# An RWKV block on one core: three products of k and v move from GpSimd to VectorE, and the written order changes

## The chip, the core and the metric

The kernel runs on one core of one Trainium2 chip. A core has five engines that run side by side, each with a queue of its own that it works off in order: TensorE (PE in the profile; its weight loads are PEld), VectorE (DVE), ScalarE (ACT), GpSimd (POOL) and SyncE (SP), which here only issues DMA transfers. They wait for one another by semaphores. SBUF holds the tiles, PSUM what TensorE writes. The metric is the device time of one execution in microseconds (us); the median of the runs counts.

## The reference

One layer of an RWKV block over 8 batches of 256 tokens and 512 channels (32 heads of 16), in float32. Cut to what matters:

```python
xn = _ln(x, ln1_w, ln1_b)
sx = _token_shift(xn, state[:, i1])
...
x5 = xn[:, :, None] + sx[:, :, None] * (maa_stack + xxx)
w = exp(-exp(time_decay + tanh(x5[:, :, 1] @ decay_w1) @ decay_w2))
r, k, v = x5[:, :, 3] @ Wr.T, x5[:, :, 0] @ Wk.T, x5[:, :, 2] @ Wv.T
g = silu(x5[:, :, 4] @ Wg.T)

def step(s, rkvw):
    r_t, k_t, v_t, w_t = rkvw
    a = k_t[:, :, :, None] * v_t[:, :, None, :]
    out = einsum('bhk,bhkd->bhd', r_t, u * a + s)
    return (a + w_t[:, :, :, None] * s, out)

_, outs = scan(step, s0, (r, k, v, w))
att = group_norm(outs) * gn_w + gn_b
x = x + att * g @ Wo.T
...
x = x + sigmoid(xr @ ffn_Wr.T) * (square(relu(xk @ ffn_Wk.T)) @ ffn_Wv.T)
```

Each head carries a state of 16 x 16 values through the 256 tokens. The outer product `a` of k and v is what the change is about.

## The kernel before, in words

The work of a batch is cut into three stages. `inputs_of_scan` loads and normalizes x, mixes it with its shifted copy into the five inputs `x5` (tiles `mix`), and projects them to r, k, v, g and the decay w. `scan` runs the recurrence. `rest` normalizes the result, projects it with Wo and runs the second half of the layer. The last part of `rest` of one batch, the scans of the next and the projections of the one after that overlap in time.

`scan` works in 4 blocks of 128 channels, and each block in 4 steps, so 16 scans a batch and 128 in all. For each step a tile `vs` of 128 x 1024 is made: SyncE loads the v of a quarter of the block, spread over the partitions, from a copy `vo` of v in DRAM (L426); ScalarE puts the starting state into its first column (L964); VectorE multiplies it by k (L971). k is read from PSUM, where ScalarE has copied it (`kp`, L952). Then VectorE runs the recurrence over the 1024 columns in one scan instruction (L973), which reads the decay `wrep` that ScalarE has spread into PSUM (L954; there is one such buffer) and writes `st`. GpSimd multiplies `st` by r (L976), and when all four steps of a block are done, TensorE sums them over the channels in 16 small matmuls (L984, the gather of the block; its output is `pat`), and VectorE adds that to `att` (L990).

In batch 0 one product by k of each block but the first, that of the fourth step, is made by GpSimd instead (L968), which reads k from SBUF. These are the three of the title.

The order of the work is written out by hand. Each operation of each stage has a number, its place in one order over all engines, in the table `TURNS` of the class `Plan`: one row for the constants, 8 rows for the stage `inputs_of_scan`, 8 for `scan`, 8 for `rest`. `sequence` gives the numbers to the operations in the order in which the stage adds them, and `order` issues them by number, takes free buffers from the pools, and sorts by the start that it works out. For one engine the order of issue is so the order of the numbers.

`tiles` chooses how matmuls whose mode is `any` are cut: in four strips of 32 columns next to operations that need such strips (mode `columns`), otherwise whole. Other operations need tiles of 32 or 64 rows, or whole ones (`turn`). A change of the mode costs TensorE something, and so does a change between the activation tables of ScalarE (`exp` and `tanh`), for which the kernel issues a load (L1131).

Names in the text: `psd0` is the output of the projection to decay and gate inputs of batch 0, `psv0_0` that of the first half of v of batch 0, `xh` a normalized x before it is turned (L616), `xin` the input of the first mixing projection (L674 its half on ScalarE), `sx` the difference of x and its shifted copy, `cm` the mean of the state.

```python
for op in self.ops:
    for b in op.bufs:
...
while queue:
    op = self.ops[heapq.heappop(queue)[1]]
    at = max([free[op.engine], op.ready] + [b.since for b in op.bufs])
...
done.sort(key=lambda op: op.start)
```

Of the kernel before, what the change touches and what calls it, by code (L numbers as in the profile page):

```python
# [71 lines left out]
class Plan:  # L72
# [61 lines left out]
    def stage(self):  # L134
# [6 lines left out]
        17 61 12 44 62 72 60 96 59 114 112 113 228 73 13 16 22 25 109 131 132 149 21 18 38 41 42 46 40 45 70 39 43 47 69  # L141
        71 74,
        0 2 1 4 3 5 6 7 8 9 26 27 34 37 52 54 31 32 36 49 28 29 33 35 50 51 30 55 56 65 53 67 68 79 103 105 125 107 108
        136 80 82 85 106 134 139 75 76 78 87 84 86 120 77 81 83 133 135 140 130 100 126 137 138 127 129 157 160 161 187
        190 141 150 158 221 224 225 147 148 153 156 151 152 201 102 104 117 119 116 123 124 128 175 197 199 163 165 176
        236 237 240 269 299 335 256 257 275,
        10 11 15 14 19 23 20 24 48 89 88 90 92 93 94 142 91 95 97 110 155 144 146 164 174 177 183 191 194 238 245 263
        265 282 246 259 261 283 243 260 266 329 244 248 258 330 202 223 226 232 252 205 206 209 254 203 219 220 281 204
        207 208 345 300 306 331 328 336 397 399 403 413 414 301 302 339 309 312 332 340 343 344 351 355 380 349 352 348
        363 387 334 341 360 415 419 444 388 389 398 358 369 372 478 480 483 404 405 416,  # L150
        66 99 101 111 121 122 143 145 154 162 159 166 181 182 186 210 167 180 188 189 200 214 227 249 218 231 251 268
        284 406 429 431 436 449 420 421 434 459 450 451 462 487 428 433 441 460 373 374 383 386 443 378 381 392 458 375
        382 385 457 376 377 384 442 481 482 486 492 494 642 650 652 654 656 580 587 602 484 500 519 532 536 539 561 590
        594 535 537 540 556 557 498 511 526 639 641 657 499 523 527 589 640 669 648 649 755 683 695 746,
        603 618 631 632 633 634 635 637 645 646 647 658 684 686 694 696 655 675 679 680 685 705 711 718 692 717 725 736
        756 759 773 775 795 807 766 772 778 782 765 776 780 781 767 770 771 845 803 809 810 828 871 805 823 827 903 804
        808 817 821 818 819 820 822 898 907 908 910 911 1013 1021 1025 1053 1062 961 1003 1005 921 922 941 943 970 971
        957 999 1055 949 952 956 958 960 843 844 869 930 946 967 962 987 1018 855 878 879 1097 1103 1118 1058 1063 1099,
        672 697 693 701 706 708 721 722 739 814 863 865 870 895 923 815 937 963 1019 1020 1023 1059 745 935 959 1006
        1009 1054 1064 1060 1078 1079 1065 1077 1080 1119 1120 1149 1173 1174 1185 1221 1172 1183 1191 1210 1162 1167  # L160
        1168 1193 1170 1188 1190 1216 1127 1130 1139 1142 1233 1134 1136 1137 1220 1128 1132 1135 1152 1129 1131 1133
        1153 1282 1299 1301 1284 1294 1326 1333 1369 1357 1372 1283 1287 1302 1303 1304 1307 1305 1313 1319 1315 1320
        1327 1306 1317 1308 1318 1328 1202 1215 1244 1247 1253 1260 1340 1346 1354 1322 1341 1347 1390 1397 1428 1349
        1350 1424,
        1029 1138 1171 1187 1207 1217 1218 1229 1241 1243 1254 1263 1264 1281 1325 790 1331 1335 1348 1374 1378 1391
        1178 1330 1334 1370 1380 1387 1405 1410 1415 1435 1407 1408 1429 1438 1444 1500 1501 1505 1511 1566 1521 1523
        1527 1587 1515 1518 1535 1551 1517 1519 1528 1550 1455 1461 1464 1479 1565 1456 1457 1469 1475 1458 1463 1470
        1473 1460 1465 1480 1549 1599 1613 1615 1604 1612 1639 1642 1643 1644 1652 1626 1641 1649 1650 1672 1698 1667
        1668 1728 1743 1745 1796 1669 1671 1675 1677 1811 1561 1562 1600 1583 1625 1635 1670 1715 1716 1619 1624 1636
        2044 2046 2047 2036 2038 2087,  # L170
        1337 1336 1338 1339 1342 1520 1524 1525 1530 1552 1553 1554 1588 1590 1614 1559 1620 1648 1651 1689 1694 1699
        1433 1621 1640 1661 1662 1688 1702 1706 1707 1720 1714 1719 1722 1738 1741 1781 1793 1823 1843 1859 1794 1800
        1806 1821 1790 1795 1797 1820 1799 1804 1819 1861 1753 1767 1771 1779 1801 1772 1773 1780 1802 1754 1758 1759
        1832 1757 1761 1762 1860 1916 1919 1920 1933 1934 2013 2014 2015 2016 2043 1883 1884 1886 1839 1848 1851 1964
        1966 1972 1971 1975 2124 1965 1973 1995 2012 2078 1857 1867 1876 1954 1963 1981 1911 1915 1922 1987 2010 2042
        2190 2191 2205 2364 2374 2398,
        1679 1629 1695 1709 1710 1712 1717 1792 1831 1835 1856 1872 1874 1918 1921 1765 1930 1936 1937 1939 1949 1978
        1784 1924 1979 2003 2037 2040 2056 1982 2033 2045 2060 2061 2077 2080 2083 2092 2094 2101 2112 2131 2097 2100
        2110 2153 2096 2109 2119 2132 2095 2111 2127 2213 2134 2143 2155 2174 2231 2136 2140 2142 2186 2135 2137 2138
        2152 2139 2168 2177 2215 2247 2248 2250 2249 2252 2281 2293 2307 2291 2292 2253 2280 2282 2314 2339 2410 2479  # L180
        2482 2484 2487 2492 2503 2483 2485 2490 2494 2515 2171 2172 2192 2318 2321 2325 2254 2258 2276 2337 2368 2381
        2525 2530 2567 2519 2520 2540,
        58 63 98 185 253 267 276 277 286 287 293 294 307 308 278 279 285 288 295 296 297 298 313 168 172 169 170 171 173
        211 192 195 196 198 280 178 179 184 193 216 213 215 217 234 255 289 320 270 229 230 233 273 290 239 262 264 315
        322 235 242 250 310 311 212 222 247 274 291 325 326 346 241 305 321 292 316 318 327 356 271 303 317 324 354 272
        304 319 323 357 314 333 347 362 367 390 391 366 353 365 368 393 412 337 342 370 394 423 338 350 364 371 395 359
        379 396 411 424 438 447,
        57 64 118 427 425 439 544 545 553 562 564 568 570 574 546 547 554 555 558 565 566 573 591 361 418 432 400 426
        440 455 497 402 430 485 495 510 401 417 435 456 509 409 461 488 496 513 531 596 514 422 504 507 515 551 464 493
        506 517 548 463 505 508 549 550 410 452 479 563 572 588 620 599 445 559 567 530 560 576 595 612 604 606 608 621  # L190
        665 524 552 571 592 629 569 593 597 611 664 666 690 644 627 663 667 691 700 609 636 643 660 676 605 607 661 671
        689 529 638 659 677 699 730 731,
        408 437 453 764 747 824 866 867 880 883 884 888 893 917 885 886 887 904 905 914 915 916 919 534 682 710 703 714
        749 753 760 623 681 698 723 748 715 716 729 750 751 724 738 752 754 763 842 936 789 651 707 709 847 873 787 791
        801 846 872 768 774 796 800 813 737 757 779 825 874 920 940 944 662 864 881 851 868 875 901 912 848 849 876 894
        896 853 882 891 933 934 786 909 928 945 953 997 998 964 929 931 955 965 966 889 926 975 1011 1034 890 1001 1012
        1017 1044 950 974 976 977 1015 1045 1046,
        850 892 980 1022 948 1024 1036 1037 1042 1047 1048 1049 1051 1071 1206 1234 1235 1236 1237 1238 1239 1249 1072
        906 1008 1032 972 984 1031 1086 1094 1028 1033 1038 1085 1125 942 1026 1030 1039 1095 994 1004 1087 1088 1144
        1146 1147 1092 1052 1084 1096 1100 1111 1073 1102 1107 1154 1211 1091 1098 1106 1176 1212 1090 1101 1105 1110  # L200
        1186 1225 1268 1256 973 1198 1199 1184 1200 1205 1209 1258 1108 1208 1227 1231 1259 1195 1222 1228 1271 1274
        1181 1182 1204 1226 1285 1321 1329 1272 1232 1273 1278 1293 1323 1214 1240 1277 1355 1360 1158 1223 1275 1290
        1316 1230 1261 1276 1361 1362 1363 1379,
        1201 1279 1314 1384 1381 1385 1388 1389 1392 1393 1400 1401 1406 1420 1522 1539 1546 1555 1556 1557 1563 1598
        1452 1248 1356 1373 1265 1386 1412 1413 1449 1280 1351 1365 1411 1447 1345 1359 1367 1382 1448 1344 1352 1366
        1375 1431 1476 1478 1445 1376 1394 1414 1477 1548 1377 1436 1439 1450 1474 1395 1441 1442 1516 1558 1396 1440
# [1001 lines left out]
```

## Time and profile before

| | before |
|---|---|
| median of 3 runs | 605.23 us (605.15 to 607.45) |
| the profiled execution | 606.28 us |
| its span from the first to the last instruction | 604.5 us |
| TensorE busy | 594.1 us (98%) |
| VectorE busy | 537.9 us (89%) |
| ScalarE busy | 517.4 us (86%) |
| GpSimd busy | 508.5 us (84%) |
| transfers | 128.07 MB, mean 212 GB/s |
| table loads of ScalarE, line 1131 | 43 |

A row of the profile gives a line of the kernel (L973 is line 973), an engine, an operation, the tiles that it writes and reads, and times. In a timeline the first number is the start and the second the time up to the end of the last of the instructions that are merged in the row; the bracket is the idle time of the engine ahead of it and what ended it. Instructions on one engine overlap a little: the next starts before the one ahead has written its last columns. The granted clock of TensorE was 1.00 in all of the span, the higher of its two levels, 2.4 GHz.

### The profile page before, as it was taken

Reading aid. Unit: us, or ns where it says so; the run is one execution under the profiler, and the core shown is the slowest. Engines: PE = TensorE matmul, PEld = TensorE weight load, DVE = VectorE, ACT = ScalarE, POOL = GpSimd, SP = SyncE. Lnnn points to the kernel's source line nnn. Section 1 sums busy time; section 2 is a strip of 40 time slices with the busy share of each in tenths; the row PEclk is TensorE's granted clock in tenths of the full one; section 3 lists DMA queues with packets and bytes.
Section 4 is the critical chain, followed back from the end, with each engine's and each line's share of the span. In section 5 each row is a group of like instructions: output and inputs, shape, how many; then the busy total and the mean of one; then the engine's idle time right before and its main releaser. Section 6 shows DMA issues by size and latency. Waiting matters only on the chain.

```text
span 604.5 us, 19879 instructions
## 1 busy us (share of the span) xinstructions
PE 594.1 (98%) x8356; PEld 344.1 (57%) x8356; DVE 537.9 (89%) x500; ACT 517.4 (86%) x1207; POOL 508.5 (84%) x390
## 2 busy tenths in 40 slices
PE   8999999999999999999999999999999999999997
PEld 7576755466446754366653755465554464455464
DVE  5789999999999999998978999999999999995342
ACT  5898879999999899999999996999999989965440
POOL 1589999989999988999979997999999989897030
PEclk9999999999999999999999999999999999999999
DMA  9895677888999679959787897785999896945352
GB/s 301 280 249 137 170 184 198 238 209 219 233 267 264 190 220 226 241 133 265 193 243 206 255 280 204 186 213 127 281 230 206 233 255 188 275 152 174 93 187 71
DMA packets 55497, 128.07 MB, mean 212 GB/s; under 512 B 6112, under 2 KB 13680, under 8 KB 55408
## 3 DMA queue, kind: packets, MB, share of 16 engines
q1 hardware_dynamic: 51040, 122.61, 74.8%
q10 hardware_dynamic: 4368, 4.20, 2.1%
q8 instruction: 65, 1.06, 0.8%
q14 instruction: 24, 0.20, 0.1%
HBM read 118.39 MB, written 8.40 MB: 210 GB/s over the span
## 4 chain that ended last, share of the span: by engine, by line
PE 86%; ACT 6%; DVE 6%; issue 1%; DMA 0%; POOL 0%; ACTq 0%; DVEq 0%; POOLq 0%
PE ps L437 73%; PE ps L984 8%; DVE st L973 2%; PE ps L848 2%; PE ps L632 2%; DVE vs L971 1%; ACT ps L796 1%; ACT L1131 1%; DVE st L600 1%; ACT sq L1039 1%; PE ps L1010 1%; ACT rk L1039 1%; DMA sq<-in_x 0%; DVE mix L798 0%; PE ps L926 0%
## 5 line engine op out<-in xcount | busy, mean ns | idle before, releaser
L973 DVE TENSOR_TENSOR_SCAN st<-wrep,vs 128x1024 f32<-128x1024 f32 x128 | 288.9, 2276 | 2.1 <-ACT wrep L954 1.1
L976 POOL TENSOR_TENSOR st<-st,r 128x1024 f32<-128x1024 f32 x128 | 254.7, 2006 | 8.3 <-DVE st L973 7.8
L971 DVE TENSOR_TENSOR vs<-vs,ps 128x1024 f32<-128x1024 f32 x125 | 147.5, 1205 | 8.7 <-ACT vs L964 6.6
L437 PE MATMUL ps<-Ws,mix 128*32 128x512 f32 (+3 forms) x836 | 115.6, 585 | 0.2 <-issue 0.2
L808 POOL TENSOR_TENSOR mix<-mix,xn 128x512 f32<-128x512 f32 x62 | 66.6, 1096 | 12.7 <-DVE mix L802 7.7
L437 PEld LDWEIGHTS ps<-Ws,mix 128*32 128x32 f32 (+1 forms) x836 | 41.2, 118 | 60.9 <-issue 49.5
L984 PE MATMUL ps<-st,con 128*32 128x256 f32 x1024 | 63.3, 380 | 0.3 <-POOL st L976 0.3
L437 PE MATMUL ps<-mix,Wr 128*32 128x256 f32 (+1 forms) x832 | 60.5, 380 | 0.7 <-issue 0.6
L437 PE MATMUL ps<-mix,Wk 128*32 128x256 f32 (+1 forms) x880 | 61.1, 380 | 0.1
L437 PE MATMUL ps<-mix,Wv 128*32 128x256 f32 (+1 forms) x832 | 60.3, 380 | 0.0
L437 PE MATMUL ps<-mix,Wg 128*32 128x256 f32 (+1 forms) x904 | 59.5, 380 | 0.0
L437 PE MATMUL ps<-mix,Ws 128*32 128x256 f32 (+1 forms) x928 | 59.3, 380 | 0.0
L437 PE MATMUL ps<-Ws,g 128*32 128x512 f32 (+1 forms) x464 | 57.3, 592 | 1.3 <-POOL g L1050 1.3
L1131 ACT ACT_TABLE_LOAD x43 | 55.2, 1283 | 1.1 <-ACT v L879 0.4
L676 POOL TENSOR_TENSOR mix<-mix,xn 128x512 f32<-128x512 f32 x44 | 47.4, 1093 | 7.5 <-ACT mix L674 7.3
L437 PEld LDWEIGHTS ps<-mix,Wk 128*32 128x32 f32 (+1 forms) x880 | 39.5, 114 | 17.8 <-issue 2.3
L984 PEld LDWEIGHTS ps<-st,con 128*32 128x32 f32 x1024 | 35.7, 110 | 23.7 <-issue 3.2
L437 PEld LDWEIGHTS ps<-mix,Wv 128*32 128x32 f32 (+1 forms) x832 | 38.9, 116 | 17.8 <-issue 2.0
L437 PEld LDWEIGHTS ps<-mix,Wr 128*32 128x32 f32 (+1 forms) x832 | 38.4, 116 | 18.6 <-issue 1.9
L934 ACT COPY att<-ps 32x256 f32<-32x256 f32 x128 | 46.6, 364 | 2.2 <-POOL g L1050 0.3
L437 PEld LDWEIGHTS ps<-mix,Ws 128*32 128x32 f32 (+1 forms) x928 | 36.0, 113 | 21.0 <-ACT mix L1065 0.8
L437 PEld LDWEIGHTS ps<-mix,Wg 128*32 128x32 f32 (+1 forms) x904 | 36.6, 113 | 19.5 <-issue 0.8
(134 smaller groups left out, 941.0 us busy)
## 6 DMA issues: line engine op xcount, KB each, us to landing
vs<-vo SPq DMA_DIRECT2D x128, 512.0 KB, 6.0
Ws<-in_fk SPq DMA_DIRECT2D x16, 512.0 KB, 6.0
Ws<-in_fr SPq DMA_DIRECT2D x16, 512.0 KB, 6.0
Ws<-in_wo SPq DMA_DIRECT2D x16, 512.0 KB, 6.4
Ws<-in_fv SPq DMA_DIRECT2D x16, 512.0 KB, 4.2
x<-in_x SPq DMA_DIRECT2D x11, 512.0 KB, 6.7
vo<-v ACTq DMA_DIRECT2D x15, 256.0 KB, 3.3
out<-o SPq DMA_DIRECT2D x15, 256.0 KB, 5.4
```

What stands on the lines that cost most here:

```text
L437: nc.tensor.matmul(out[i : i + n], lhsT=w[:, i : i + n], rhs=x, start=first, stop=final)
L632: nc.tensor.transpose(ps()[:, m, n * P : (n + 1) * P], xh[n]()[:, k * P : (k + 1) * P], idt())
L676: gp(512, t, [t, xn[q]], lambda q=q, t=t: nc.gpsimd.tensor_tensor(t(), t(), xn[q]()[:, :, 1 : T + 1], ALU.add))
L808: gp(512, t, [t, xn[q]], lambda q=q, t=t: nc.gpsimd.tensor_tensor(t(), t(), xn[q]()[:, :, 1 : T + 1], ALU.add))
L848: nc.tensor.matmul(pd()[i : i + 32, 0, :], lhsT=w, rhs=src[k // 2]()[:, k % 2, :], start=(k == begin), stop=(k == end))
L934: act(350, atts[q], [pc], lambda i=32 * (2 * q + m), m=m, q=q, h=32 * h: nc.scalar.copy(atts[q]()[h : h + 32, m, :], pc()[i : i + 32, 0, :]))
L971: dve(4 * T, [vs], [vs, kp], lambda m=m, vs=vs, kp=kp: nc.vector.tensor_tensor(vs(), vs(), kp()[:, m : m + 1, :].to_broadcast([P, 4, T]), ...
L973: dve(4 * T, [st], [w, vs], lambda w=w, vs=vs, st=st: nc.vector.tensor_tensor_scan(st().rearrange("p n t -> p (n t)"), w().rearrange("p n ...
L976: gp(4 * T, st, [st, r], lambda m=m, st=st, r=r: nc.gpsimd.tensor_tensor(st(), st(), r()[:, m : m + 1, :].to_broadcast([P, 4, T]), ALU.mul ...
L984: nc.tensor.matmul(pat()[32 * i : 32 * i + 32, 0, :], lhsT=con()[:, s : s + 32], rhs=done[i]()[:, j, :], start=(j == 0), stop=(j == 3),)
L1039: act(256, rsb, [rs], lambda blk=2 * q + n, n=n, rows=rows, rsb=rsb: nc.scalar.copy(by_block(rsb)[rows, n, :], rs()[32 * blk : 32 * blk + ...
L1131: nc.scalar.preload_act_table_set(TABLES[table])
```

## The change

The condition for GpSimd's product becomes one that no block fulfils (there are blocks 0 to 3), so VectorE makes all 128 products by k. The table of turns has new numbers in all its rows, as many as before. The diff, cut to the condition, the row of the constants, the row of `inputs_of_scan` of batch 0 and that of `scan` of batch 0:

```diff
@@ -138,130 +138,131 @@
     TURNS = """
-        17 61 12 44 62 72 60 96 59 114 112 113 228 73 13 16 22 25 109 131 132 149 21 18 38 41 42 46 40 45 70 39 43 47 69
-        71 74,
-        0 2 1 4 3 5 6 7 8 9 26 27 34 37 52 54 31 32 36 49 28 29 33 35 50 51 30 55 56 65 53 67 68 79 103 105 125 107 108
-        136 80 82 85 106 134 139 75 76 78 87 84 86 120 77 81 83 133 135 140 130 100 126 137 138 127 129 157 160 161 187
-        190 141 150 158 221 224 225 147 148 153 156 151 152 201 102 104 117 119 116 123 124 128 175 197 199 163 165 176
-        236 237 240 269 299 335 256 257 275,
...
-        58 63 98 185 253 267 276 277 286 287 293 294 307 308 278 279 285 288 295 296 297 298 313 168 172 169 170 171 173
-        211 192 195 196 198 280 178 179 184 193 216 213 215 217 234 255 289 320 270 229 230 233 273 290 239 262 264 315
-        322 235 242 250 310 311 212 222 247 274 291 325 326 346 241 305 321 292 316 318 327 356 271 303 317 324 354 272
-        304 319 323 357 314 333 347 362 367 390 391 366 353 365 368 393 412 337 342 370 394 423 338 350 364 371 395 359
-        379 396 411 424 438 447,
...
+        10 34 12 33 35 102 93 100 104 92 107 103 188 78 14 15 17 21 57 58 59 66 19 13 30 23 49 50 20 52 64 41 44 45 63
+        65 67,
+        0 3 1 2 4 5 6 7 9 8 18 27 38 43 47 48 26 28 29 68 16 22 31 36 42 46 53 54 55 56 60 61 62 69 96 97 117 108 109
+        118 70 71 91 123 124 149 72 87 94 105 110 119 131 73 74 90 127 145 147 153 128 129 136 137 138 139 146 163 164
+        168 171 132 135 144 210 214 231 140 152 156 182 151 157 197 99 111 112 113 114 122 125 126 186 202 205 155 169
+        190 229 230 238 273 292 295 265 266 268,
...
+        106 116 143 221 262 270 271 274 281 282 283 285 288 294 284 286 287 319 332 333 334 345 297 159 165 130 160 162
+        166 195 158 172 176 198 212 161 184 187 199 211 174 204 213 220 256 272 307 234 189 232 233 237 299 175 218 236
+        301 316 207 251 255 260 290 206 253 258 305 310 331 336 368 217 280 309 315 317 337 339 369 267 289 304 322 349
+        261 296 306 321 341 291 302 308 338 367 395 396 373 356 360 364 398 405 324 344 361 409 423 323 325 365 377 394
+        351 352 378 414 440 444 447,
...
@@ -964,7 +965,7 @@
                 act(4, vs, [s0, cm], lambda i=i, blk=blk, vs=vs: nc.scalar.activation(
                     vs()[:, :, 0:1], s0()[:, blk, 4 * i : 4 * i + 4].rearrange("p (n o) -> p n o", o=1),
                     AF.Identity, bias=cm()[:, blk : blk + 1]), pointers=1)
-                if i == 3 and b == 0 and blk:
+                if i == 3 and b == 0 and blk > 9:
                     gp(4 * T, vs, [vs, k], lambda m=m, vs=vs, k=k: nc.gpsimd.tensor_tensor(
                         vs(), vs(), k.place[:, m : m + 1, 1 : T + 1].to_broadcast([P, 4, T]), ALU.mult), 1.815)
```

The places of the operations that the prediction speaks of, read by counting through the rows of the two tables:

| operation | place before | place after |
|---|---|---|
| TensorE, `psv0_0`, first piece | 102 | 99 |
| TensorE, `psd0`, first piece | 100 | 128 |
| ScalarE, half of `xin` of batch 1, first and second | 144, 146 | 133, 170 |
| ScalarE, `xh` of batch 2 (L616), the later one | 162 | 167 |
| ScalarE, copy of k of batch 0 into PSUM (L952) | 168 | 159 |
| ScalarE, first `wrep` (L954) | 172 | 165 |
| VectorE, first product, first scan | 171, 173 | 162, 166 |
| VectorE, last scan of batch 0 | 411 | 414 |
| TensorE, last gather of batch 0 | 438 | 444 |
| VectorE, last scan of batch 1 | 691 | 697 |
| TensorE, last gather of batch 1 | 730 | 723 |

## Rows read from the trace of the kernel before

**Rows 1.** The page's first part: span, then busy time, share and instructions of each engine.

```profile
span 604.5 us, 19879 instructions
...
PE 594.1 (98%) x8356; PEld 344.1 (57%) x8356; DVE 537.9 (89%) x500; ACT 517.4 (86%) x1207; POOL 508.5 (84%) x390
```

**Rows 2.** Windows: stretch, length, busy us of each engine, clock, DMA.

```profile
0.00:33.70 33.70, 30.00 (x374) 22.52 (x375) 21.30 (x55) 24.92 (x60) 12.44 (x24) 1.00 0.89 286
33.70:160.00 126.30, 124.36 (x2042) 79.53 (x2043) 125.61 (x101) 115.26 (x274) 121.06 (x86) 1.00 0.80 200
160.00:555.00 395.00, 393.83 (x5748) 217.05 (x5744) 375.54 (x315) 358.33 (x843) 368.77 (x276) 1.00 0.81 220
555.00:604.50 49.50, 45.90 (x207) 25.00 (x196) 15.43 (x30) 18.86 (x33) 6.25 (x6) 1.00 0.38 128
```

**Rows 3.** Waits of TensorE: total us, times, longest.

```profile
PE ps L437 <- POOL g L1050: 1.3, 1, 1.3
```

**Rows 4.** Timeline of VectorE, 28 to 125: start, us, instructions.

```profile
32.38 1.22 DVE L971 TENSOR_TENSOR vs<-vs,ps 128x1024 f32<-128x1024 f32 x1 [3.19 <-ACT vs L964]
33.71 2.29 DVE L973 TENSOR_TENSOR_SCAN st<-wrep,vs 128x1024 f32<-128x1024 f32 x1
...
77.17 3.47 DVE L971 TENSOR_TENSOR vs<-vs,ps 128x1024 f32<-128x1024 f32 x3
80.56 2.28 DVE L973 TENSOR_TENSOR_SCAN st<-wrep,vs 128x1024 f32<-128x1024 f32 x1
...
85.47 6.64 DVE L973 TENSOR_TENSOR_SCAN st<-wrep,vs 128x1024 f32<-128x1024 f32 x3
```

**Rows 5.** Timeline of GpSimd, around the last factors of three blocks.

```profile
88.15 6.03 POOL L976 TENSOR_TENSOR st<-st,r 128x1024 f32<-128x1024 f32 x3
...
151.10 3.97 POOL L976 TENSOR_TENSOR st<-st,r 128x1024 f32<-128x1024 f32 x2
...
167.16 2.00 POOL L976 TENSOR_TENSOR st<-st,r 128x1024 f32<-128x1024 f32 x1 [0.18 <-DVE st L973]
```

**Rows 6.** Timeline of TensorE, the gathers of the same three blocks.

```profile
94.24 1.91 PE L984 MATMUL ps<-st,con 128*32 128x256 f32 x26 [0.31 <-POOL st L976]
...
155.53 1.91 PE L984 MATMUL ps<-st,con 128*32 128x256 f32 x32
176.45 1.91 PE L984 MATMUL ps<-st,con 128*32 128x256 f32 x32
```

**Rows 7.** Instructions on tile vs: ns shortest/median/longest, first and last start, forms.

```profile
L971 DVE TENSOR_TENSOR vs<-vs,ps x125: 1183/1209/1222, 32.4 to 544.0; 128x1024 f32<-128x1024 f32 x125
L968 POOL TENSOR_TENSOR vs<-vs,k x3: 2025/2406/2431, 44.2 to 85.8; 128x1024 f32<-128x1024 f32 x3
```

**Rows 8.** Timeline of ScalarE ahead of the first scan.

```profile
25.91 1.28 ACT L1131 ACT_TABLE_LOAD   x1
...
28.02 0.51 ACT L674 ACTIVATE mix<-sx,vec 128x256 f32<-128x256 f32 x1 [0.52 <-POOL sx L657]
28.43 0.19 ACT L576 ACTIVATE rs<-rs 128x2 f32<-128x2 f32 x1
28.52 0.49 ACT L674 ACTIVATE mix<-sx,vec 128x256 f32<-128x256 f32 x1
28.92 0.56 ACT L879 COPY k<-ps 128x512 f32<-128x512 f32 x1
...
30.82 0.81 ACT L616 ACTIVATE xh<-x,nm,rs 128x512 f32<-128x512 f32 x1
31.52 0.59 ACT L952 COPY ps<-k 128x512 f32<-128x512 f32 x1
...
32.23 1.02 ACT L954 ACTIVATE wrep<-w 128x1020 f32<-128x1020 f32 x1
```

**Rows 9.** Chain that ended last, in order of time: start, us, what.

```profile
143.48 1.86 PE ps L984 x32
...
155.71 1.73 PE ps L984 x32
```

227 rows, old and new, of the table TURNS are left out of this document.

## The prediction

> **What bounds the kernel now.** I read the summary of the page first. The program fills 604.5 us, and TensorE is busy for 594.1 of them, far ahead of VectorE's 537.9, ScalarE's 517.4 and GpSimd's 508.5 [rows 1]. A TensorE this full can only be helped by removing matmul time or idle time, and the matmuls are the same on both sides of the diff. So I went to the windows, to see where its idle lies: 3.70 us before 33.70, 1.94 from there to 160, 1.17 from 160 to 555 and 3.60 after [rows 2]. First and last are the ramp and the end of the last batch. What a better order could win between them is 1.94 + 1.17 = 3.11 us. Among TensorE's waits, the longest in that part is 1.3 us for `g` from GpSimd [rows 3], and one of 0.3 us is for `st`, from GpSimd too [rows 6].
>
> The second thing to see in the windows is VectorE. Between 33.70 and 160 it is busy for 125.61 of 126.30 us, as full as TensorE; after 160 it has 395.00 - 375.54 = 19.5 us to spare [rows 2]. GpSimd, from which work is taken, has 5.24 us idle in the first stretch [rows 2]. So the change loads the engine that has no room just there.
>
> The timeline shows how tightly the two engines run. VectorE starts the first product of the scans at 32.38 after 3.19 us idle, the first scan at 33.71, and the last scan of batch 0 ends at 85.47 + 6.64 = 92.11 [rows 4]. GpSimd multiplies the last result by r, ending at 88.15 + 6.03 = 94.18 [rows 5], and TensorE waits with the gather of that block until 94.24 [rows 6]. The last gather of batch 1 starts at 155.53, and its last factor is there at 151.10 + 3.97 = 155.07: 0.46 us of room. Only the next one, first of batch 2, has room: ready at 169.16, run at 176.45 [rows 5, 6]. Until 155, what is late on VectorE is late on TensorE.
>
> **Part 1: three products move.** GpSimd's three took 2.03, 2.41 and 2.43 us (shortest, median, longest), 6.87 in all. VectorE's own 125 took between 1.18 and 1.22 [rows 7], and behind one another they cost less, because the next starts before the last one is written: from 77.17 three of them were started in the 3.39 us up to the scan at 80.56, 1.13 each [rows 4]. Both kinds read and write the same shapes, and VectorE's form, with k in PSUM, is the one it already runs; so the term is 3 x 1.13 = 3.39 us, with 3 x 1.22 = 3.66 as its upper bound. What hides it would be idle time of VectorE, of which there are 0.69 us between 33.70 and 160 [rows 2].
>
> Could the new turns hide it by sending other VectorE work behind the scans? I compared, in both tables of turns, what stands ahead of each batch's scans. Ahead of the last scan of batch 0, one half of `x5` (a multiplication of 512 columns) goes out and the three products come in. Ahead of the last scans of blocks 2 and 3 of batch 1, and of the first block of batch 2, VectorE has the same operations as before and the three products. TensorE has the same work ahead of the last gather of batch 1 in both. So nothing is sent away, and the 3.39 us stay.
>
> **Part 2: an earlier start of the scans.** The new turns change the queue of ScalarE ahead of the first scan. Before, between the table load at 25.91 and the spread decay `wrep` at 32.23, it waits 0.52 us for GpSimd's `sx`, does two halves of `xin` (28.02 to 28.43 and 28.52 to 28.92) and an `xh` (30.82 to 31.52) [rows 8]. In the new order one of these halves (place 144 to 133) stands ahead of that table load, in time in which ScalarE waits for TensorE's `psd0`; the other (146 to 170) and the `xh` (162 to 167) stand behind `wrep` (172 to 165). That takes away 0.52 + 0.41 + 0.40 + 0.70 = 2.03 us; a small negation of `cm` comes in, for which I take 0.13. The scan starts about 1.9 us earlier. v is projected before `psd0` now (99 against 102, while `psd0` goes from 100 to 128), so that its copy through DRAM is no later. The bounds are 0, if w or the spread v is not there sooner, and 2.03. I take 1.9, since the rows show ScalarE without a gap from 28.02 on, so that the queue set the time. Until the last gather of batch 1 this leaves 3.39 - 1.9 = 1.49 us of lag on VectorE, of which 0.46 us are room: TensorE is 1.03 us later there. The lag at 94 (3.39 less one `x5` half and less 1.9) is part of this sum and not a second term.
>
> The row shows a VectorE with no room and a GpSimd with some [rows 2]. [...]
>
> **Part 3: changes of tile shape.** Counted over the two orders, TensorE changes between its ways of tiling (32 columns, 32 rows, 64 rows, whole) 73 times before and 70 times after. What one costs: a gather takes 1.86 us where it follows matmuls of another shape and 1.73 where not [rows 9], 0.13. Three fewer give 0.39 us, all on TensorE's path. ScalarE has 41 table loads for 43 (1.28 us each [rows 8]); it is not the bound, and I give them nothing: ScalarE's spare time hides them.
>
> **Part 4: all the other turns.** From 160 to 555 nearly every row of the table has new numbers. Nothing in the trace prices them one by one. What they can win there is the 1.17 us of idle; what they can lose I bound by the idle rate of the stretch before 160, 1.94 us in 126.30, over 395 us: 6.07, that is 4.9 more than now. I take 0: VectorE's 19.5 us of room there is nearest to the rows as they stand. The transfers are the same in number; `vs` waits for a free buffer, which a scan gives back.
>
> **The sum.** +1.03 - 0.39 = +0.64 us on TensorE's path. The profiled execution took 606.28 us, so it would be 606.9. The median of the runs is 605.23, 1.05 below that execution; I forecast the median: 605.9 us.
>
> **The rivals.**
> No earlier start: w or the spread v holds the first scan at 33.71. Then +3.39 - 0.46 - 0.39 = +2.5, 607.8. For it: 0.52 us of ScalarE's idle belongs to another engine. Against it: the unbroken queue [rows 8].
> Hidden: the lag falls into waits that are there already (0.3 and 1.3 us in the same stretch [rows 3, 6]), and only the shape changes count: -0.39, 604.8. Against it: those waits hang on the same scans.
> Faster: GpSimd is the real pace of the first batches. Its queue loses 6.87 us before 88.2, the waits for `g` and `st` go, and with them TensorE's idle up to 555: -3.11 - 0.39 = -3.5, 601.7. The point from which it decides is a first scan 3.39 - 0.46 = 2.9 us earlier, before 30.8. For it: the longest wait names GpSimd. Against it: VectorE's 0.69 us of idle.
> Slower: the new turns of 160 to 555 leave gathers ahead of their factors, as the gathers up to 155 stand now; at the idle rate of the first stretch, +4.9 + 0.64 = +5.5, 610.8. It is over 0.5% once the idle there grows by some 2.4 us. For it: VectorE enters this stretch later. Against it: 7 us of room at 176.45 [rows 5, 6].
>
> **How the numbers follow.** I give the forecast 0.32 (its own range 605 to 607), no earlier start 0.20, hidden 0.15, faster 0.13, slower 0.20. A measurement of this kernel tells about 0.5%, 3 us, from no change. The first three lie within it: 0.67; faster 0.13; slower 0.20. The range reaches toward the two outer rivals until about 0.1 is left out on either side: 602.5 to 609.5.
>
> **What would show it.** Right: 128 products on VectorE near 1.21 us and none on GpSimd; a first scan near 31.8; the last scan of batch 0 near 93 and its gather waiting until about 95; the last gather of batch 1 near 156.5; TensorE idle from 160 to 555 about 1.2 us. Wrong: a first scan at 33.7 or before 30.8; a last gather of batch 1 earlier than 155; or more than 3 us of TensorE idle behind 160, which I hold to be the weakest place of this forecast.

## The result and the profile after

| | before | after |
|---|---|---|
| median of 7 runs each | 606.10 us (605.15 to 609.72) | 610.03 us (607.46 to 611.63) |
| mean of the same runs | 606.70 us | 609.59 us |
| ratio | | 1.0047, interval 1.0026 to 1.0068 |
| the profiled execution, its span | 606.28, 604.5 us | 610.06, 608.3 us |

The change makes the kernel slower by 0.47%, or 2.9 us of 606.7; the forecast was +0.64 us. (The medians lie 3.9 us apart; the means and the repetition in experiment 8 say 2.9 to 3.0.) One execution among all that follow, of kernel 10, took 888.46 us at a granted clock of 0.655, and is in no number below. The sum of the page and the windows of the kernel after, with the columns of [rows 1, 2]:

```profile
span 608.3 us, 19418 instructions
...
PE 593.1 (98%) x8140; PEld 343.6 (56%) x8140; DVE 540.9 (89%) x503; ACT 514.9 (85%) x1205; POOL 502.2 (83%) x387
```

```profile
0.00:33.70 33.70, 28.98 (x322) 22.57 (x322) 21.01 (x56) 24.68 (x58) 10.59 (x22) 1.00 0.87 275
33.70:160.00 126.30, 121.76 (x1961) 75.84 (x1963) 124.50 (x100) 113.28 (x269) 113.92 (x82) 0.99 0.79 199
160.00:555.00 395.00, 392.62 (x5600) 218.03 (x5596) 378.76 (x318) 360.58 (x849) 367.79 (x277) 1.00 0.81 220
555.00:608.30 53.30, 49.72 (x276) 27.20 (x268) 16.59 (x32) 16.35 (x31) 9.86 (x8) 1.00 0.37 129
```

TensorE's idle time is 4.72, 4.54, 2.38 and 3.58 us in the four stretches, where it was 3.70, 1.94, 1.17 and 3.60: most of the loss is made before 160 us. VectorE, which was given work, shows more idle time in the second stretch than before (1.80 against 0.69 us). The longest waits of TensorE between 33.7 and 165 us (line waiting, engine and line waited for, total, times, longest):

```profile
PE ps L438 <- ACT k L880: 1.5, 1, 1.5
PE ps L985 <- ACT r L880: 1.0, 1, 1.0
PE ps L438 <- DVE mix L799: 0.8, 1, 0.8
```

The wait for `g` of [rows 3] is gone, and two waits for copies by ScalarE, 2.5 us together, are new. VectorE's timeline, at the places of [rows 4], and the gathers of [rows 6] in TensorE's:

```profile
31.09 1.22 DVE L972 TENSOR_TENSOR vs<-vs,ps 128x1024 f32<-128x1024 f32 x1 [0.54 <-ACT vs L965]
32.59 2.29 DVE L974 TENSOR_TENSOR_SCAN st<-wrep,vs 128x1024 f32<-128x1024 f32 x1 [0.27 <-ACT wrep L955]
...
83.83 1.20 DVE L972 TENSOR_TENSOR vs<-vs,ps 128x1024 f32<-128x1024 f32 x1
...
89.26 4.46 DVE L974 TENSOR_TENSOR_SCAN st<-wrep,vs 128x1024 f32<-128x1024 f32 x2
```

```profile
95.64 1.93 PE L985 MATMUL ps<-st,con 128*32 128x256 f32 x31
...
115.97 0.69 PE L438 MATMUL ps<-tb,mw2b 32*64 32x256 f32 x16 [1.52 <-ACT k L880]
117.65 3.34 PE L985 MATMUL ps<-st,con 128*32 128x256 f32 x32 [0.99 <-ACT r L880]
...
159.30 1.94 PE L985 MATMUL ps<-st,con 128*32 128x256 f32 x32
...
180.10 1.91 PE L985 MATMUL ps<-st,con 128*32 128x256 f32 x32
```

The first scan comes 1.12 us earlier, at 32.59. The last scan of batch 0 ends at 93.72, 1.61 us later than before, and its gather runs at 95.64, later by 1.40. The last gather of batch 1 is at 159.30, later by 3.77, that of the first block of batch 2 by 3.65, and the last gather of all, at 558.3 against 554.6, by 3.7: what is lost by 160 us is carried to the end and grows no more. GpSimd's last factor of batch 1 (answer to [rows 5]) and all products by k (answer to [rows 7]):

```profile
155.14 3.97 POOL L977 TENSOR_TENSOR st<-st,r 128x1024 f32<-128x1024 f32 x2
```

```profile
L972 DVE TENSOR_TENSOR vs<-vs,ps x128: 1194/1212/1222, 31.1 to 545.8; 128x1024 f32<-128x1024 f32 x128
```

That factor is ready at 159.11 and its gather starts at 159.30, so there is as little room as before. ScalarE ahead of the first scan, for [rows 8]:

```profile
26.42 1.28 ACT L1132 ACT_TABLE_LOAD   x1
...
28.37 0.59 ACT L880 COPY k<-ps 128x512 f32<-128x512 f32 x1
28.85 0.82 ACT L617 ACTIVATE xh<-x,nm,rs 128x512 f32<-128x512 f32 x1
29.57 0.59 ACT L953 COPY ps<-k 128x512 f32<-128x512 f32 x1
30.62 0.30 ACT L965 ACTIVATE vs<-s,cm 128x4 f32<-128x4 f32 x1 [0.46 <-DMA vs<-vo]
30.82 0.82 ACT L872 ACTIVATE w<-ps,vec 128x256 f32<-128x256 f32 x2
31.53 1.02 ACT L955 ACTIVATE wrep<-w 128x1020 f32<-128x1020 f32 x1
```

The halves of `xin` and the later `xh` are gone from this queue, as the diff says, but its table load ends 0.51 us later than before (27.70 against 27.19), and it now waits 0.46 us for the transfer of `vs`. The chain that ended last again has a dearer and a cheaper gather, as in [rows 9]; the dearer one was 1.86 before:

```profile
148.93 1.93 PE ps L985 x32
159.51 1.73 PE ps L985 x32
```

### The profile page after: what moved, and what is told of

It reads as the page before. It is cut to its first block, busy times and chain, and to the rows that moved or that the text cites. A ratio compares the mean times of both kernels' runs of the same rounds, so it can differ in the third digit from the quotient of the medians.

```text
span 608.3 us, 19418 instructions
## 1 busy us (share of the span) xinstructions
PE 593.1 (98%) x8140; PEld 343.6 (56%) x8140; DVE 540.9 (89%) x503; ACT 514.9 (85%) x1205; POOL 502.2 (83%) x387
## 4 chain that ended last, share of the span: by engine, by line
PE 76%; ACT 11%; DMA 5%; DVE 4%; issue 2%; SPq 1%; POOL 0%; ACTq 0%; DVEq 0%
PE ps L438 64%; PE ps L985 8%; DMA vs<-vo 3%; DVE st L974 2%; PE ps L849 1%; ACT L1132 1%; PE ps L633 1%; DMA Ws<-in_wv 1%; ACT att L935 1%; ACT ps L797 1%; ACT wrep L955 1%; DMA vo<-v 1%; ACT sq L1040 1%; DVE vs L972 1%; ACT att L1046 1%
## 5 line engine op out<-in xcount | busy, mean ns | idle before, releaser
L972 DVE TENSOR_TENSOR vs<-vs,ps 128x1024 f32<-128x1024 f32 x128 | 151.0, 1209 | 4.9 <-ACT vs L965 4.1
L438 PE MATMUL ps<-mix,Wk 128*32 128x256 f32 (+1 forms) x856 | 58.9, 379 | 0.0
L658 POOL TENSOR_TENSOR sx<-xn 128x512 f32<-128x512 f32 x22 | 23.1, 1060 | 39.1 <-ACT xn L654 39.1
L438 PEld LDWEIGHTS ps<-mix,Wg 128*32 128x32 f32 (+1 forms) x784 | 39.4, 118 | 18.2 <-issue 2.8
L438 PEld LDWEIGHTS ps<-mix,Wk 128*32 128x32 f32 (+1 forms) x856 | 37.5, 115 | 19.3 <-issue 1.8
```

The costliest lines, as they stand in the source:

```text
L438: nc.tensor.matmul(out[i : i + n], lhsT=w[:, i : i + n], rhs=x, start=first, stop=final)
L658: take(512, [sx], [xn], lambda xn=xn, sx=sx, e=nc.vector if alone and q else nc.gpsimd: e.tensor_tensor(sx(), xn()[:, :, 0:T], xn()[:, :, ...
L972: dve(4 * T, [vs], [vs, kp], lambda m=m, vs=vs, kp=kp: nc.vector.tensor_tensor(vs(), vs(), kp()[:, m : m + 1, :].to_broadcast([P, 4, T]), ...
```

## The experiments

Two readings stood against each other: that VectorE's 3.4 us of products set the loss (the prediction), and that it comes from what else the diff moves, the order and the buffers that go with it. In the table, the ratio is to runs of the kernel before on the same chip (medians there 605.6 to 606.0); first scan and last gather of batch 1 are starts in the trace of one execution. Such a start is good to some 0.7 us: of kernels with the same order up to there, those with the old one start the first scan between 33.71 and 34.46, those with the new one between 32.00 and 32.69. The traces of kernels 7 and 11 stand apart: their granted clock was 0.91 over the first 20 us, 1.00 in all the others.

| kernel | median us | ratio (interval) | first scan | last gather b. 1 |
|---|---|---|---|---|
| before | 605.6 to 606.0 | 1 | 33.71 | 155.5 |
| 1 old order, products on VectorE | 610.87 | 1.0087 (1.0066 to 1.0107) | 34.25 | 161.6 |
| 2 new order, products on GpSimd | 615.86 | 1.0156 (1.0131 to 1.0180) | 32.0 | 163.6 |
| 3 after, gather moved up | 611.12 | 1.0089 (1.0064 to 1.0114) | 32.49 | 159.6 |
| 4 old ramp, new rest | 609.03 | 1.0059 (1.0037 to 1.0080) | 33.83 | 160.0 |
| 5 new ramp, old rest | 615.63 | 1.0164 (1.0146 to 1.0181) | 32.69 | 165.8 |
| 6 old order, narrow products | 608.26 | 1.0040 (1.0025 to 1.0054) | 34.31 | 158.5 |
| 7 new order, narrow products | 609.26 | 1.0054 (1.0032 to 1.0076) | 33.55 | 159.5 |
| 8 after, again | 609.08 | 1.0049 (1.0031 to 1.0066) | 32.56 | 159.3 |
| 9 old order and buffers, VectorE | 608.48 | 1.0043 (1.0025 to 1.0062) | 34.46 | 159.6 |
| 10 old order and buffers, narrow | 606.06 | 1.0009 (0.9990 to 1.0028) | 34.01 | 156.1 |
| 11 after, k from SBUF | 611.20 | 1.0093 (1.0063 to 1.0123) | 33.60 | 160.9 |
| 12 after's buffers, GpSimd | 614.32 | 1.0151 (1.0122 to 1.0180) | 32.58 | 164.6 |

**1 and 2: the two halves of the diff, each alone.** Kernel 1 has the old table of turns and the new condition, kernel 2 the new table and the old condition:

```diff
-                if i == 3 and b == 0 and blk:
+                if i == 3 and b == 0 and blk > 9:
```

```diff
-                if i == 3 and b == 0 and blk > 9:
+                if i == 3 and b == 0 and blk:
```

> The old table of turns, and all products of batch 0 on VectorE. If the three products are what costs (3 x 1.13 = 3.39 us on a VectorE that is full until 160), it is 2 to 3.4 us slower than the kernel before, as the changed kernel is (2.8). If the new turns are what costs, it is within 1 us of the kernel before.

> The new table of turns, and the three products on GpSimd as before. If the products cost, VectorE is 3.39 us shorter and the kernel is within 1 us of the one before. If the new turns cost (a ramp that is 1.0 us late at 40, the waits of 1.5 and 1.0 us around 116), it stays 2 to 3.5 us slower.

Both lose more than the whole change does, and more than either expectation allowed: +5.3 and +9.4 us against +2.9. So the halves aren't a sum; the new order gives back some 2 us of what the products cost in the old one, and it counts on them being on VectorE. But +5.3 is more than three products of 1.2 us can make. Two waits of TensorE between 80 and 97 us in kernel 1 are not in the kernel before:

```profile
86.36 1.93 PE L988 MATMUL ps<-st,con 128*32 128x256 f32 x32 [1.34 <-DVE mix L802]
...
95.00 1.12 PE L441 MATMUL ps<-ta,mw2a 32*64 32x256 f32 x32 [2.09 <-DVE vs L975]
```

A gather that waits for a mix, and a mixing matmul that waits for a product by k, do not read these results. They wait for a PSUM buffer. Experiments 6 and 9 take this up.

**3: the waits near 116 us.** The changed kernel, with these places changed in its table: the copies of r and v of batch 2 on ScalarE stand ahead of the spread decay of the second block of batch 1 (520 and 516 to just ahead of 507), the gather of batch 1's first block ahead of the mixing matmul that waited for the copy of k (528 to just ahead of 524).

> The changed kernel with three operations in other places: the first gather of batch 1 ahead of the mixing matmul that needs four PSUM buffers, and ScalarE's copies of r and v of batch 2 ahead of the second spread decay. If the waits of 1.52 and 0.99 us around 116 are a loss of their own, most of them go and it is 2 us faster than the changed kernel. If they only show VectorE's lag, TensorE waits later instead and it gains under 0.7 us.

The two waits for copies go, the wait for `g` from GpSimd comes back and grows to 2.81 us, and the time is no better. The row of TensorE in kernel 3:

```profile
121.82 1.50 PE L441 MATMUL ps<-Ws,g 128*32 128x512 f32 x12 [2.81 <-POOL g L1054]
```

So taking these two waits away is worth nothing by itself. It suggests, and does not show, that several chains are late at this place and the order only chooses for which of them TensorE waits.

**4 and 5: is it the ramp?** All products on VectorE; the places until about the first scan are of one table and the rest of the other (for kernel 5 with `before` and `after` exchanged):

```
key = (0, place_before) if place_before <= 203 else (1, place_after)
```

> All products on VectorE; the first 204 places (about the first 40 us) in the old order, then the new order. If the later ramp (TensorE 1.0 us behind at 40) is a loss of its own, it is about 1 us faster than the changed kernel; if VectorE's load sets the time, the scans start 1.1 us later again and it is up to 1.1 us slower.

> All 128 products on VectorE; places 0 to 203 (until about the first scan) in the new order, the rest in the old. Theory A (the earlier first scan is what the new order wins back): the first scan begins near 32.6 us as in the changed kernel, and the time falls from the 610.9 us of the products in the old order to about 609 us, as much as the first scan comes earlier. Theory B (the order behind the first scan wins it back, the start does not): 610.5 us or more, whatever the first scan does.

Kernel 4 starts its first scan at 33.83, 1.2 us later than the changed kernel, and takes as long (609.03 against 609.08 in experiment 8). Kernel 5 starts it 1.6 us earlier than kernel 1 and takes 4.8 us longer; behind its ramp VectorE waits for ScalarE:

```profile
DVE mix L802 <- ACT ps L800: 6.3, 3, 3.8
```

So no worth of the earlier first scan shows in the new order. The bound is wide, though: by the ratios kernel 4 is 0.6 us slower than kernel 8, give or take 1.7, and in the traces its last gather of batch 1 is 0.7 us later, so that a part of the 1.2 us may be worth something. Kernel 5 gives theory B its number but does not price the start: it joins two orders that were not made for each other, and what it loses in these waits hides whatever the start may win. What wins some 2 us back from kernel 1 is then the order behind the first scan, which kernel 4 has. And the 1.0 us that TensorE idles more ahead of 33.70 in the changed kernel does not show as its loss either, since kernel 4 has the old ramp (3.41 us idle there) and is no faster.

**6, 7 and 8: the products almost for nothing.** In the old order (6) and in the new one (7), each of the three products is cut to 32 of its 1,024 columns, and the scan takes the other columns without k; 8 is the changed kernel without an edit, on the same chip.

```diff
                 if i == 3 and b == 0 and blk:
-                    gp(4 * T, vs, [vs, k], ...
+                    dve(4 * T, [vs], [vs, kp], lambda m=m, vs=vs, kp=kp: nc.vector.tensor_tensor(
+                        vs()[:, :, 0:8], vs()[:, :, 0:8], kp()[:, m : m + 1, 0:8].to_broadcast([P, 4, 8]), ALU.mult))
```

> The old order; each of the three products of the first batch is narrowed to 32 of its 1,024 columns on VectorE, so that neither VectorE nor GpSimd pays for them (the other columns go into the scan without k). Theory A (the order is fitted to these products on GpSimd and VectorE's load in the first batch sets the time): VectorE's work up to 160 us is as before, so 605 to 606 us. Theory B (GpSimd's three products of 1.8 us held something up in the kernel before): 603 us or less.

> The new order with the same three narrow products. Theory A (the 3.4 us of the products on VectorE's full first batch are the whole loss of the change): the loss goes, 605 to 606 us, no slower than the kernel before. Theory B (the new order itself loses time, in the waits of 1.5 and 1.0 us near 116 us): 608 us or more, as the changed kernel.

> The changed kernel once more, on the same chip as the three kernels above, for comparison: 608 to 610 us where the kernel before has 605.5 us.

Neither theory of experiment 6 had this: with less work on VectorE than in kernel 1 and less on GpSimd than before, the old order still loses 2.3 us (608.26). (GpSimd's products took 2.0 to 2.4 us each [rows 7], not the 1.8 of the expectation.) The same two waits of TensorE are there, the second one now for a product of 0.16 us:

```profile
84.37 1.93 PE L988 MATMUL ps<-st,con 128*32 128x256 f32 x32 [1.15 <-DVE mix L802]
...
91.97 1.12 PE L441 MATMUL ps<-ta,mw2a 32*64 32x256 f32 x32 [1.06 <-DVE vs L972]
```

In the new order, taking some 3.1 us off VectorE gains nothing (609.26 against 609.08), and the waits near 116 us stay as long. In kernel 7:

```profile
116.67 0.69 PE L441 MATMUL ps<-tb,mw2b 32*64 32x256 f32 x16 [1.50 <-ACT k L883]
118.35 3.02 PE L988 MATMUL ps<-st,con 128*32 128x256 f32 x32 [0.99 <-ACT r L883]
```

So in the changed kernel the load of VectorE is not what sets the time of batch 1. (The profiled execution of kernel 7, 613.25 us, is the longest of its nine: its first scan comes 1.0 us later than in kernel 8, behind the lower clock of its ramp, and it lost some 3 us more around 300. So the medians carry this, and the trace only the waits.)

**9 and 10: the same engine, other buffers.** `order` gives a tile the free buffer that was given back last, by the starts that it works out:

```python
b.slot = max((s for s in self.pools[b.pool] if s[0] <= at), key=lambda s: s[0])
```

VectorE's product reads the PSUM copy `kp` of k, GpSimd's reads k in SBUF. With the three products on VectorE, the copy of the last two blocks of batch 0 (`kp0_1`) stays in use until the very last product, and the allocation, followed through the code, gives 12 PSUM tiles another predecessor. In the kernel before, the gather's output `pat0_2` takes the buffer of `kp0_1`; in kernels 1 and 6 it takes one that a mix (`psm2_3_1`) gives back, and a mixing matmul (`psm2_1_0`) takes that of `kp0_1`. These are the two waits. Kernel 9 lets `order` allocate as before and changes the engine; with it the product's place in VectorE's queue changes, since `order` still plans it for GpSimd: the last one stands ahead of the last two scans of batch 0, where kernel 1 has it ahead of the last one. Kernel 10 narrows the product as well (`vs()[:, :, 0:8]` times 8 columns of k).

```diff
-                    gp(4 * T, vs, [vs, k], lambda m=m, vs=vs, k=k: nc.gpsimd.tensor_tensor(
+                    gp(4 * T, vs, [vs, k], lambda m=m, vs=vs, k=k: nc.vector.tensor_tensor(
                         vs(), vs(), k.place[:, m : m + 1, 1 : T + 1].to_broadcast([P, 4, T]), ALU.mult), 1.815)
```

> The kernel before in its order and with its buffers, tile by tile; only the engine of the three products changes (VectorE, which reads k from SBUF as GpSimd did, so that the PSUM copy of k is let go as early as before). Theory A (part of the loss of the products in the old order, 2.3 us that the narrow products kept, is PSUM buffers given in another rotation and held until the last product): 608.3 to 608.9 us, the products' own time on VectorE alone. Theory B (VectorE's time is all of it, the buffers do nothing): 610.9 us as with the products moved in the old order.

> As the kernel with the kept buffers, and the three products narrowed to 32 of 1,024 columns. Theory A (buffers): 605.5 to 606.2 us, the kernel before, since VectorE's work and the buffers are those of before. Theory B: 608.3 us as the narrow products in the old order had it. If it falls below 605 us, GpSimd's three products cost something in the kernel before.

Theory A held in both: 608.48 and 606.06 us. The narrow kernel is back at the kernel before, within its interval, and its gather and matmul no longer wait:

```profile
82.85 1.91 PE L984 MATMUL ps<-st,con 128*32 128x256 f32 x32
...
89.31 1.12 PE L437 MATMUL ps<-ta,mw2a 32*64 32x256 f32 x32
```

Kernel 1's +5.3 us come apart: the products, +2.8 (kernel 9 against its own runs of before, 605.69; 2.4 against kernel 10), and the buffers, 610.87 - 608.48 = 2.4. The narrow pair gives the buffers by themselves, since the place of a product of 0.16 us costs nothing: 608.26 - 606.06 = 2.2, by the ratios 1.9 with a bound of 0.4 to 3.3. And kernels 1 and 6, alike in order and buffers, give the products by themselves, with k in PSUM: 610.87 - 608.26 = 2.6. The experiments do not tell whether the copy that is held longer or the other rotation makes the buffers' part. GpSimd's products held up nothing that shows: without them, kernel 10 is no faster than the kernel before, within about 1 us.

**11 and 12: the buffers of the changed kernel.** Its order and its allocation; the three products read k from SBUF, on VectorE (11) or on GpSimd (12, `nc.gpsimd` in the same place):

```diff
+                elif i == 3 and b == 0 and blk:
+                    dve(4 * T, [vs], [vs, kp], lambda m=m, vs=vs, k=k: nc.vector.tensor_tensor(
+                        vs(), vs(), k.place[:, m : m + 1, 1 : T + 1].to_broadcast([P, 4, T]), ALU.mult))
                 else:
```

> The changed kernel, its order and its buffers; the three products read k from SBUF, so nothing waits for them to let go of the PSUM copy of k. Theory A (the held copy costs in the new order too): 607 us or less. Theory B (the new order gives that buffer to a tile that comes late enough, the hold costs nothing there): 609 us, as the changed kernel.

> The changed kernel's order and buffers, with the three products on GpSimd as before the change (from k in SBUF). Theory A (the loss of the new order with the products on GpSimd, 615.9 us, came mostly of the PSUM buffers that it was given): 609 us or less. Theory B (GpSimd's products come late where the new order counts on VectorE's): 613 us or more.

Kernel 11 fits neither number: it is 2 us slower than the changed kernel in experiment 8. Letting go of `kp0_1` wins nothing that shows. That fits a new order that has the last product of batch 0 at 83.83 us already (93.75 in kernel 1), but it is no clean test, since two of the products became longer, for a reason told at the end. Kernel 12 went as theory B: with the changed kernel's buffers, GpSimd's products still cost 5 us more than VectorE's. In its trace TensorE waits for a factor that stands behind a product in GpSimd's queue, and VectorE waits 5.99 us for that gather:

```profile
68.93 2.02 POOL L972 TENSOR_TENSOR vs<-vs,k 128x1024 f32<-128x1024 f32 x1
70.88 2.02 POOL L980 TENSOR_TENSOR st<-st,r 128x1024 f32<-128x1024 f32 x1
```

```profile
72.96 2.12 PE L988 MATMUL ps<-st,con 128*32 128x256 f32 x27 [2.03 <-POOL st L980]
```

No version ran that beats the kernel before.

## Why the prediction was right and wrong

The time lay in its range and, at +0.47%, just within "no change"; the sum was too small by 2.9 - 0.64 = 2.3 us. Of the signs that it named, the last gather of batch 0 came as said (about 95, measured 95.64), that of batch 1 did not (near 156.5, measured 159.30): the account failed between the two.

**Part 1, the products.** Right in kind and size in the old order: 3.39 us less 0.46 of room is 2.93, where kernel 1 against kernel 6 shows 2.6 and kernel 9 lost 2.8 (interval of the ratio: 1.5 to 3.8 us). What it didn't see is that the same move in the old order costs 2 us more through PSUM. The sentence that failed is that both kinds read and write the same shapes, so that the term is VectorE's time: the operands lie in other memories, and the one in PSUM is a buffer that another tile waits for. In the order that the change brings, even VectorE's time did not show as a cost: without 3.1 us of it kernel 7 is as slow as kernel 8, give or take 1.7 us.

**Part 2, the earlier start: the credit that failed.** The first scan came 1.12 us earlier in this pair of traces and not 1.9: the prediction took ScalarE's queue as what set the time. From the end of the table load to `wrep` that queue became 1.21 us shorter (5.04 to 3.83), 0.46 us of waiting for `vs` included, but the table load ended 0.51 us later. More than the size, the use of it was not borne out. The 1.9 us were taken off the lag at 155 us one for one; kernel 4, with the old start, takes as long as the changed kernel, within its bound of 1.7 us. Without that credit the prediction's own sum is 3.39 - 0.46 - 0.39 = +2.5, which was the rival "no earlier start", 607.8 against 605.23, and near the measured +2.9. That nearness is luck too: the scan did start earlier, and the 3.39 us that make this sum are those that kernel 7 took away in vain.

**VectorE as the pace until 155.** This is the step that failed: "Until 155, what is late on VectorE is late on TensorE." It held in the old order, where VectorE's products moved the last gather of batch 1 by 4.1 us in kernel 9 against 0.6 in kernel 10. In the new one kernel 7 took them away, and neither the time (609.26 against 609.08) nor the gather (159.5) came earlier. There TensorE waits for PSUM buffers that copies of ScalarE give back: neither waiting matmul reads k or r, and followed through the code, the mixing matmul at 115.97 takes the buffer of `psk2_1` and the gather at 117.65 that of `psr2_0`, the projections that ScalarE copies to k and r of batch 2. Kernel 3's order gives that gather another buffer, that of `kp1_0`, and is no faster. In the changed kernel's trace ScalarE runs from 106.81 to 121 almost without a gap, with two table loads where the kernel before has one in the same stretch:

```profile
107.64 1.28 ACT L1132 ACT_TABLE_LOAD   x1
...
111.66 1.28 ACT L1132 ACT_TABLE_LOAD   x1
...
114.85 0.59 ACT L880 COPY v<-ps 128x512 f32<-128x512 f32 x1
115.33 0.59 ACT L880 COPY k<-ps 128x512 f32<-128x512 f32 x1
```

The matmul at 115.97 starts as the copy of k ends. That wait shows which engine TensorE waits for, and the chain that ended last agrees: from 99.60 to past 120 nearly all its pieces are ScalarE's, which has 11% of the whole chain where it had 6% in the kernel before. It does not show that a shorter queue of ScalarE would win the time back: kernel 3 took the copies out of the way and waited for `g` instead. No run relieved ScalarE there without moving other work, so the last cause of these 2.5 us stays open.

**Part 3, tile shapes and table loads.** A gather behind matmuls of another shape takes 1.93 us in the chain (1.86 before), one behind its own shape 1.73 as before. A gain of 0.39 us can't be seen: TensorE's busy time is 592.2 us in kernel 3, with the new shapes, and between 592.2 (kernel 1) and 594.1 (before) with the old. That table loads cost nothing is not contradicted by their number over the span, 41 for 43; whether it holds for the two that stand ahead of the copies now, no run shows.

**Part 4, the turns after 160: right within its bound.** TensorE's idle time there grew to 2.38 us from 1.17 (it is 1.36 in experiment 8), below the 3 us named as the limit, and the lag at the gathers, 3.77 us at 159.3, is 3.7 at the last one. The slower rival, which rested on this stretch, did not happen.

**The clock.** The sum has no term for TensorE's granted clock. In 13 of 18 executions of the changed kernel its mean lies below 0.999, and these took some 2 us longer than the other five (told at the end).

**The direction of the move.** The Trainium skill (Perfetto Trace Analysis, Optimizing Scalar/DVE Operations) says that where VectorE is saturated, handing work to ScalarE or even to GpSimd may make sense. The old order agrees: moving products to VectorE cost 2.8 us at equal buffers (kernel 9) and 5.3 as it came (kernel 1). The new order does not: with the products back on GpSimd it takes 5 us more (kernel 12 against kernel 8).

## What to carry to other kernels

When an operation changes its engine, price its operands' buffers as well as its time: reading k from PSUM some ten us later cost about as much in the old order as the products' own time on a full engine. An order that was fitted by hand, its buffers and the placing on engines belong together, so test each with the others held (same order and same allocation, then only the engine), because halves taken apart cost 5.3 and 9.4 us where the whole cost 2.9. An earlier start is not worth its size at the end by itself; look for the next wait before crediting it. And compare executions by their granted clock as well as by their time.

## What the hardware showed unexpectedly

**VectorE and GpSimd get in each other's way when VectorE reads two operands from SBUF.** In kernel 11 the three products read `vs` and k from SBUF. All tiles `vs` in its trace (ns shortest, median, longest):

```profile
L975 DVE TENSOR_TENSOR vs<-vs,ps x125: 1187/1211/1223, 32.1 to 547.8; 128x1024 f32<-128x1024 f32 x125
...
L972 DVE TENSOR_TENSOR vs<-vs,k x3: 1195/2039/2467, 55.6 to 86.8; 128x1024 f32<-128x1024 f32 x3
```

The 125 with k in PSUM never take over 1.22 us, though GpSimd is busy for 83% of the span. Of the other three, two take 2.04 and 2.47 us. The longest started at 67.26, in the middle of the first of two instructions of GpSimd; the short one started at 86.76, and there GpSimd's two `rk` took 3.14 us, where 16 such instructions in the changed kernel take 1.09 to 1.10 each:

```profile
67.26 2.47 DVE L972 TENSOR_TENSOR vs<-vs,k 128x1024 f32<-128x1024 f32 x1
...
86.76 1.20 DVE L972 TENSOR_TENSOR vs<-vs,k 128x1024 f32<-128x1024 f32 x1
```

```profile
66.64 4.95 POOL L980 TENSOR_TENSOR st<-st,r 128x1024 f32<-128x1024 f32 x2
```

```profile
85.76 3.14 POOL L922 TENSOR_TENSOR rk<-r,k 128x512 f32<-128x512 f32 x2
```

GpSimd's two factors from 66.64 on took longer as well, 4.95 us where two such take 3.97 [rows 5]. So the engines hold each other up. The Trainium skill (SBUF — State Buffer, Who interferes with whom) says that a VectorE instruction with two inputs in SBUF contends with a GpSimd instruction that reads SBUF, and that the order of issue decides which of the two is blocked. The trace agrees: 2.47 us in place of 1.20 for the product that came second, 3.14 in place of 2.2 for the pair of which one `rk` came second. The two longer products make (2.04 - 1.21) + (2.47 - 1.21) = 2.1 us more, about what kernel 11 lost to the changed kernel, which is an agreement of sizes and not a proof, the less so as kernel 7 won nothing by 3.1 us less on VectorE. It is also what the copy of k in PSUM is good for. In kernel 9, whose products read SBUF too, all three took 1.20 to 1.22, and there it was GpSimd that was held: the factor that it began during the last product took 2.84 us (2.00 in kernel 10), and two at the second product 4.77 in place of 3.97. GpSimd stood idle behind both, 0.48 and 1.29 us, so this need not have cost kernel 9 anything.

```profile
90.69 1.20 DVE L968 TENSOR_TENSOR vs<-vs,k 128x1024 f32<-128x1024 f32 x1
```

```profile
90.91 2.84 POOL L976 TENSOR_TENSOR st<-st,r 128x1024 f32<-128x1024 f32 x1 [2.97 <-DVE st L973]
```

**The granted clock fell once within the span.** Behind the wait of 1.52 us the changed kernel's TensorE ran a while at the lower level; the window after it, with the columns of [rows 2]:

```profile
112.00:116.50 4.50, 2.98 (x64) 1.43 (x56) 4.50 (x4) 4.41 (x8) 4.50 (x4) 1.00 1.04 323
116.50:120.50 4.00, 3.01 (x36) 1.57 (x32) 3.43 (x4) 3.96 (x11) 3.11 (x4) 0.58 0.84 200
```

TensorE was busy for 2.98 of the 4.50 us ahead of it (4.20 in the kernel before), and then 0.58 is a mean between the higher level and the lower one, 1.2 GHz: the gather took 3.34 us in place of 1.9. Kernels 4, 7 and 8 have the same fall at this gather (3.35, 3.02 and 3.38 us); in kernel 3, without the two waits, the clock stays at 1.00, behind its wait of 2.81 us too.

How much hangs on it can be read from the mean granted clock of each execution. In experiment 8 the four at 0.999 or 1.000 took 607.2 to 608.1 us (mean 607.5) and the seven at 0.997 took 609.05 to 610.75 (mean 609.8). With the seven executions of the result it is 607.8 for five and 609.7 for thirteen. The kernel before is the same with and without a fall (605.8 and 605.9 us; 28 and 24 executions of the experiments). So about half of what an execution with a fall loses goes with the fall, and some 2 us are lost without one. This compares executions and is no experiment: where the clock fell is known from the traces alone, and a longer wait may bring both the fall and the time. Taking the waits away did not pay: kernel 3's two executions at 1.000 took 609.2 and 609.4 us.
